# Layer 1 with VectorE's instructions in source order, the closing chain and the token steps cut into pieces

## The chip, the cores and the metric

The kernel runs on one core of a Trainium2 chip. A core has four compute engines with a queue each: TensorE (PE in the profile; its weight loads are shown apart as PEld), VectorE (DVE), ScalarE (ACT) and GpSimd (POOL). SyncE (SP) issues the DMA transfers. TensorE reads operands from SBUF and writes PSUM, from where VectorE and ScalarE read. The metric is the device time of one execution of the whole program in microseconds.

## The reference

Four layers are applied to x, four images of 56 x 56 tokens with 256 channels. Each is `x = x + layer(group_norm(x))`. Layers 0, 2 and 3 are window attentions with 8 heads and are not touched. Layer 1, on the N = 3136 tokens of an image, is cut here to what matters (W_adj is diagonal):

```
xn   = x / norm(x)                              # per token
A    = exp(5 * (xn W_adj xn^T - rowmax))        # N x N, diagonal set to 0
A    = A / rowsum(A);   rowsum = sum(A)
diff = rowsum * (x W_aff + b_aff) - (A x) W_aff
y    = leaky_relu(layer_norm(diff) * gamma + beta, 0.01)
```

All is float32.

## The kernel before

`layer1` works image by image. The tokens of an image are 24 tiles of 128 (`NB`) and a rest of 64 (`REST`). They are made ready in seven chunks: six of four tiles and one for the rest (chunk 6, `NC4`). For a chunk, `tokens` returns a list of steps:

- `load`: the DMA of the chunk, two `normalise` operations on VectorE (L939, group norm, one per half of the channels), a square on ScalarE (L1368).
- `lengths`: sixteen one-column matmuls that sum the squares (L1376); VectorE clips the sum into `rn` (L1378), GpSimd raises it to the power -1/2 (L1379) and spreads it over a diagonal `dg` (L1380).
- two `values` steps: x W_aff into `xw` (L1389), evacuated by ScalarE or VectorE (L954, L952). A last column of xw holds -1, so that the same product gives the row sums.
- `unit_length`: a matmul with `dg` (L1397) and a VectorE product into `xnT` (L1399).

A is symmetric but for its normalisation, so only the blocks on and above the diagonal are computed. A unit `(b, j, first, last)` is row tile j against up to four column tiles. `logits` gives 1 to 4 tiles by matmul (L1421), ScalarE's exp (L1424) and on the diagonal a GpSimd mask (L1426); it runs one unit ahead of the products. `transposed` transposes the tiles on TensorE (L1491) and copies them on ScalarE (L1494). `products` then uses each tile twice: `by_row` (L1505) adds to row j's sum in the PSUM tile `ps_o`, `by_column` (L1510) makes the part of row i in a `ps_v` tile, of which there are two, and `add_up` adds it to `acc` in SBUF on VectorE (L1433; the first time a copy, L1436). Units whose j is None are rest units: the 64 rest tokens against 1024 tokens, with the same scheme on 64-row halves (L1443, L1462, L1472, L1476).

When row j is complete, `finish` closes it, an operation at a time: VectorE adds `ps_o` and `acc` (L1540), takes a reciprocal (L1544), combines (L1546), takes mean and variance (L1549 to L1551); GpSimd raises to a power (L1553); VectorE normalises (L1554); GpSimd applies gamma and beta (L1555, L1556); VectorE applies the leaky ReLU (L1557). It returns `add`, which transposes y on TensorE (L1562) and adds it to the residual (L1570); a full residual chunk gets its statistics (L894) and is stored.

Around the units runs a list `small`. After every unit's products `done` grows by its number of tiles, and twice per unit `small_step` runs the first entry that has come due, or a step of the group statistics. `replace` is called at seven row tiles of an image (j = 3, 6, 10, 14, 18, 20, 22) and puts a chunk of the next image into `small`: its load at once, its other steps eight tiles later. `now` runs all steps of a chunk that a unit is about to need.

`run` opens a layer under a manual schedule for a set of engines. For layer 1 that set holds TensorE alone: TensorE executes in the order of the source, and a scheduler decides how VectorE, ScalarE, GpSimd and SyncE order their own instructions. The first image's chunks are prepared in a loop ahead of the first unit. Layer 2's first loads (`layer2_ahead`) are issued during layer 1.

Of the kernel before, what the change touches and what calls it, by code (L numbers as in the profile page):

```python
# [830 lines left out]
def direct_blocks(ctx: ExitStack, tc: tile.TileContext, d: dict, watch):  # L831
# [501 lines left out]
    def layer1(early, big, pool, late, next_layer):  # L1333
# [16 lines left out]
        def tokens(b, c, ps_a=ps_m):  # L1350
# [6 lines left out]
            def load():  # L1357
                x = early.tile([P, CC, 512], FP, tag="x", name="x1")
                if c < NC4:
                    nc.sync.dma_start(out=x[:, :, :n], in_=tokens_of(1, b, 4 * c * P, n))  # L1360
                else:
                    for i in range(2):
                        nc.sync.dma_start(out=x[:, :, i * REST:(i + 1) * REST], in_=tokens_of(1, b, NB * P, REST))
                x1 = box["x"] = early.tile([P, CC, 512], FP, tag="xn", name="xn1")
                sq = box["sq"] = x
                for h in range(CC):
                    normalise(x1[:, h, :n], x[:, h, :n], known(1, b), h)
                nc.scalar.activation(sq[:, :, :n], x1[:, :, :n], AF.Square)  # L1368

            def lengths():  # L1370
                pm, sq = ps_a(), box["sq"]
                rn = early.tile([P, 4, 1], FP, tag="rn", name="rn")
                dg = box["dg"] = early.tile([P, 4, P], FP, tag="dg", name="dg", bufs=1)
                for i, t in enumerate(tiles):
                    for h in range(CC):
                        nc.tensor.matmul(pm[:k, i:i + 1], lhsT=sq[:, h, i * P:i * P + k], rhs=ones[:, 0:1],  # L1376
                                         start=(h == 0), stop=(h == CC - 1))
                nc.vector.tensor_scalar_max(rn[:k, :m, 0], pm[:k, :m], TINY * TINY)  # L1378
                nc.gpsimd.tensor_tensor(rn[:k, :m, 0], rn[:k, :m, 0], mhalf[:k, 0:1].to_broadcast([k, m]), ALU.pow)  # L1379
                nc.gpsimd.tensor_tensor(  # L1380
                    dg[:k, :m, :k], ident[:k, :k].rearrange("p (o q) -> p o q", o=1).to_broadcast([k, m, k]),
                    rn[:k, :m, :].to_broadcast([k, m, k]), ALU.mult)
# [22 lines left out]
            return [load, lengths] + [lambda i=i: values(i) for i in range(0, m, 2)] + [unit_length]  # L1405
# [23 lines left out]
        touched = set()  # L1429
# [36 lines left out]
        def rest_products(b, q, e, own, at):  # L1466
            po = psum_tile("o", 2)
            for i in range(4):
# [6 lines left out]
                for a in range(2):  # L1475
                    nc.tensor.matmul(po[a * REST:(a + 1) * REST, :C + 1], lhsT=at[:, i * P + a * REST:i * P + (a + 1) * REST],  # L1476
                                     rhs=xw[:, 8 * q + 4 * a + i, :], start=(i == 0), stop=(i == 3 and (a == 1 or own is None)))
            if own is not None:
                nc.tensor.matmul(po[:REST, :C + 1], lhsT=own, rhs=xw[:REST, NB, :], start=False, stop=True)
# [17 lines left out]
        def products(b, j, first, last, e, at):  # L1497
# [18 lines left out]
            for n, i in enumerate(others):  # L1516
                by_column(i)
                if n:
                    by_row(rows.pop(0))
            for i in rows:  # L1520
                by_row(i)
# [3 lines left out]
        def residual(b, c):  # L1525

            if (b, c) not in xr and c < NCH:
                xr[b, c] = late.tile([P, CC, CH], FP, tag="xr", name="xr1", bufs=3)
                nc.sync.dma_start(out=xr[b, c], in_=tokens_of(1, b, c * CH, CH))
            return xr.get((b, c))  # L1530

        def finish(b, j):

            n = P if j < NB else REST
            y = late.tile([P, C + 1], FP, tag="y", name="y", bufs=5) if j < NB else y_rest
# [12 lines left out]
            mv = pool.tile([P, 2], FP, tag="mv", name="mv1")  # L1548
# [3 lines left out]
            rstd = pool.tile([P, 1], FP, tag="rstd", name="rstd")  # L1552
            nc.gpsimd.tensor_tensor(rstd[:n], mv[:n, 1:2], mhalf[:n, 0:1], ALU.pow)  # L1553
            nc.vector.tensor_scalar(y, y, mv[:n, 0:1], rstd[:n], ALU.subtract, ALU.mult)  # L1554
            nc.gpsimd.tensor_tensor(y, y, gamma[:n], ALU.mult)  # L1555
            nc.gpsimd.tensor_tensor(y, y, beta[:n], ALU.add)  # L1556
            nc.vector.scalar_tensor_tensor(y, y, 0.01, y, ALU.mult, ALU.max)  # L1557

            def add():
# [5 lines left out]
                while t0 < j * P + n:  # L1565
# [9 lines left out]
                    t0 = t1  # L1575
            return add
# [16 lines left out]
        for c in range(2):  # L1593
            fresh[c].pop(0)()
        for c in range(NC4 + 1):
            for step in fresh[c]:
                step()
            if c + 2 <= NC4:
                fresh[c + 2].pop(0)()
        small, done = [], 0  # L1600

        def small_step():
            for i, (when, step, _) in enumerate(small):
                if when <= done:
                    small.pop(i)
                    return step()
            step_stats()

        def now(chunk):

            for item in [a for a in small if a[2] == chunk]:
# [3 lines left out]
        def replace(b, c):  # L1615
            if b < NIMG:
                for item in [a[2] for a in small if a[2]]:
                    now(item)
                load, *steps = tokens(b, c)
                load()  # L1620
                small[:0] = [(done + 8, step, (b, c)) for step in steps]
# [10 lines left out]
        for k, w in enumerate(units):  # L1632
# [19 lines left out]
            else:  # L1652
                products(*w, e, at)
                done += w[3] - first
                if w[3] == NB:
                    adds = [finish(b, j)] + ([last_add] if j == NB - 1 else [])
                    small += [(done + 6, add, None) for add in adds]
            e = ahead
        return [step for _, step, _ in small]
# [418 lines left out]
    with pool_of(2, 0) as early, ExitStack() as ends:  # L2078
        late = ends.enter_context(pool_of(1, 3))
        held = {}  # L2080
        last_steps = run(1, lambda own: layer1(*own, late, lambda: layer2_ahead(early, held)), {E.PE}, range(3))
# [101 lines left out]
```

## Time and profile before

| | |
|---|---|
| median of 3 runs | 4060.51 us (4051.37 to 4060.95) |
| the profiled execution | 4046.79 us, span 4044.6 us |
| layer 0 up to | about 795 us of the span |
| layer 1, first image's chunks | 795 to about 848 us |
| layer 1, units | 848 to about 2805 us |
| TensorE busy from 870 to 2803 us | 1888.64 of 1933 us |
| VectorE busy from 870 to 2803 us | 850.06 us |
| ScalarE, GpSimd busy there | 404.40, 464.02 us |
| share of DMA there | 0.06 |

In a profile line, `L1433 DVE` is an operation of VectorE at line 1433 of the kernel. A timeline line has the start, the time to the last end, the engine, the line, the operation with its tiles, the count, and in brackets the idle time of the engine ahead of it with the work that ended it. A line of waits has who waited for whom, the total in us, the number of times and the longest one. In a line of windows, the figures after the two bounds are the length, and then the busy time of PE, PEld, DVE, ACT and POOL with the number of instructions in brackets, the share of full clock that TensorE was granted, the busy share of the DMA engines and GB/s.

### The profile page before, as it was taken

How to read it: one execution, taken by the hardware profiler on the slowest of the kernel's cores; microseconds unless marked ns; L12 is line 12 of the kernel's file. 1: busy time of each engine (PE TensorE's matmuls, PEld its weight loads, DVE VectorE, ACT ScalarE, POOL GpSimd, SP SyncE). 2: the span in 40 equal slices, each digit the busy share in tenths (PEclk: the TensorE clock that was granted, in tenths of full speed). 3: DMA queues.
4: the chain of work that ended last, by engine and by line, in shares of the span. 5: the costliest groups of instructions: out<-in, count | busy, mean ns of one | idle time of the engine just before them, and what ended most of it. 6: DMA issues, size and time to landing. Idle time of an engine off the chain costs nothing.

```text
span 4044.6 us, 92225 instructions
## 1 busy us (share of the span) xinstructions
PE 3858.0 (95%) x38983; PEld 2715.6 (67%) x38983; DVE 2364.8 (58%) x4427; ACT 1375.9 (34%) x2899; POOL 1741.2 (43%) x1883
## 2 busy tenths in 40 slices
PE   6999999899999999999999999999999999999998
PEld 4566666557777577775777757776676676666665
DVE  6777777634444444444344543445788877666665
ACT  3355555322222122222222212222555555344443
POOL 2566767621123211232112321123676777545544
PEclk9899999899999999999999999999999999999999
DMA  8443333320000000000000000001444443322221
GB/s 266 102 133 121 114 118 105 104 85 6 24 23 29 25 6 24 15 29 25 6 24 15 29 19 10 10 10 50 126 128 131 125 119 113 102 73 73 74 77 62
DMA packets 241072, 276.12 MB, mean 68 GB/s; under 512 B 23430, under 2 KB 233000, under 8 KB 240168
## 3 DMA queue, kind: packets, MB, share of 16 engines
q1 hardware_dynamic: 240362, 270.06, 21.5%
q8 instruction: 308, 5.05, 0.5%
q14 instruction: 114, 0.93, 0.1%
q10 hardware_dynamic: 288, 0.08, 0.0%
HBM read 190.55 MB, written 79.53 MB: 67 GB/s over the span
## 4 chain that ended last, share of the span: by engine, by line
PE 48%; DVE 4%; POOL 2%; issue 1%; SPq 0%; DMA 0%; ACT 0%; DVEq 0%; POOLq 0%; ACTq 0%
PE ps_m L945 12%; PE ps_o L1505 6%; PE ps_s L1421 6%; PE ps_v L1510 6%; PE ps_o L1100 3%; PE ps_m L962 3%; PE ps_s L1071 3%; PE ps_o L1040 2%; PE ps_m L982 2%; PE ps_t L1491 1%; PE ps_s L1025 1%; DVE rs L1796 1%; PE ps_m L1389 1%; DVE xn L939 0%; DVE e L1078 0%
## 5 line engine op out<-in xcount | busy, mean ns | idle before, releaser
L1433 DVE TENSOR_TENSOR acc<-acc,ps_v 128x257 f32<-128x257 f32 x1104 | 455.8, 421 | 686.5 <-PE ps_v L1510 671.7
L1510 PE MATMUL ps_v<-xw,e 128*128 128x257 f32 x2208 | 613.1, 382 | 19.7 <-DVE acc L1433 18.0
L1505 PE MATMUL ps_o<-xw,at 128*128 128x257 f32 x2208 | 609.0, 379 | 0.0
L1421 PE MATMUL ps_s<-xnT,xd 128*128 128x512 f32 (+3 forms) x1344 | 571.1, 547 | 0.0
L1494 ACT COPY at<-ps_t 128x512 f32<-128x512 f32 (+3 forms) x332 | 170.5, 514 | 1049.8 <-PE ps_t L1491 1049.8
L1510 PEld LDWEIGHTS ps_v<-xw,e 128*128 128x128 f32 x2208 | 408.6, 189 | 171.1 <-issue 80.4
L1091 POOL TENSOR_TENSOR b<-e 126x336 f32<-126x336 f32 (+5 forms) x512 | 500.0, 997 | 10.0 <-ACT e L1079 1.9
L1505 PEld LDWEIGHTS ps_o<-xw,at 128*128 128x128 f32 x2208 | 419.1, 190 | 60.1
L1414 POOL TENSOR_SCALAR xd<-xnT,vec 128x128 f32<-128x128 f32 x192 | 115.1, 610 | 632.2 <-PE ps_s L1421 629.7
L945 PE MATMUL ps_m<-xn,w_wqkv 128*128 128x392 f32 x1024 | 381.6, 507 | 3.9 <-DVE xr L1831 2.5
L1082 POOL TENSOR_TENSOR e<-e,m0t 126x672 f32<-126x672 f32 (+3 forms) x128 | 238.7, 1865 | 265.0 <-ACT e L1081 252.1
L1082 POOL TENSOR_TENSOR e<-e,bias 119x784 f32<-119x784 f32 (+5 forms) x128 | 244.4, 1909 | 180.9 <-ACT e L1081 179.7
L1421 PEld LDWEIGHTS ps_s<-xnT,xd 128*128 128x128 f32 x1344 | 225.5, 191 | 134.8 <-issue 126.2
L1424 ACT ACTIVATE e<-ps_s 128x512 f32<-128x512 f32 x336 | 185.3, 551 | 336.7 <-PE ps_s L1421 336.7
L1003 ACT ACTIVATE no<-rs 128x168 f32<-128x168 f32 (+2 forms) x256 | 93.9, 367 | 590.2 <-DVE rs L1796 273.2
L945 PEld LDWEIGHTS ps_m<-xn,w_wqkv 128*128 128x128 f32 x1024 | 190.0, 192 | 127.5 <-ACT pr L2028 17.2
L1100 PEld LDWEIGHTS ps_o<-e,vp 124*32 124x32 f32 (+3 forms) x8192 | 176.3, 110 | 141.6 <-issue 93.0
L1100 PE MATMUL ps_o<-e,vp 124*32 124x112 f32 (+3 forms) x8192 | 238.8, 253 | 6.2 <-POOL e L1082 4.4
L939 DVE TENSOR_SCALAR xn<-x,gst 128x28 f32<-128x28 f32 (+5 forms) x368 | 208.1, 619 | 35.2 <-PE ps_m L945 28.7
L1079 ACT ACTIVATE e<-e 126x672 f32<-126x672 f32 (+5 forms) x256 | 219.5, 857 | 19.0 <-DVE e L1078 6.0
L1796 DVE RECIPROCAL rs<-ps_o 128x196 f32<-128x196 f32 (+2 forms) x128 | 176.0, 1375 | 77.7 <-PE ps_o L1100 77.1
L1032 POOL TENSOR_TENSOR e<-e,m3l 98x784 f32<-98x784 f32 x64 | 118.2, 1846 | 235.7 <-ACT e L1029 212.5
(197 smaller groups left out, 6340.9 us busy)
## 6 DMA issues: line engine op xcount, KB each, us to landing
x<-xr SPq DMA_DIRECT2D x64, 392.0 KB
x<-in_x SPq DMA_DIRECT2D x53, 448.0 KB
x<-x SPq DMA_DIRECT2D x60, 392.0 KB
xr<-x SPq DMA_DIRECT2D x60, 392.0 KB
vd<-v SPq DMA_DIRECT2D x48, 384.0 KB
xr<-in_x SPq DMA_DIRECT2D x32, 392.0 KB
xr<-x SPq DMA_DIRECT2D x28, 448.0 KB
x<-xr SPq DMA_DIRECT2D x28, 448.0 KB
```

The costliest lines, as they stand in the source:

```text
L939: nc.vector.tensor_scalar(dst, src, gst[:, h, 0:1], gst[:, h, 1:2], ALU.subtract, ALU.mult)
L945: nc.tensor.matmul(pm[:, :n], lhsT=w[:, h, col:col + P], rhs=rhs(h), start=(h == 0), stop=(h == CC - 1))
L1079: nc.scalar.activation(ev, ev, AF.Exp)
L1082: nc.gpsimd.tensor_tensor(parts(ev), parts(ev), w["emask"], ALU.mult)
L1091: nc.gpsimd.tensor_tensor(w["b"][a][:nk, :, :2 * nq].rearrange("p h (i c) -> p h i c", i=2), ev[:, :, :, 0, :], ev[:, :, :, 1, :], ALU.add)
L1100: nc.tensor.matmul(w["o"](k, i)[j * HD:(j + 1) * HD], lhsT=ones[:nk, :HD] if k else v(j, u), rhs=w["b"][j // 2][:nk, j % 2, i * nq:(i + 1) ...
L1421: nc.tensor.matmul(s[:, :n], lhsT=xd[j][:, h, :], rhs=xnT[:, h, first * P:last * P], start=(h == 0), stop=(h == CC - 1))
L1424: nc.scalar.activation(e[:, :n], s[:, :n], AF.Exp, scale=5.0)
L1433: nc.vector.tensor_tensor(acc[:, i, :], acc[:, i, :], pv[:, :C + 1], ALU.add)
L1505: nc.tensor.matmul(out[j][:, :C + 1], lhsT=e[:, col(i)] if i == j else at[:, col(i)], rhs=xw[:, i, :], start=(i == j), stop=(i == NB - 1))
L1510: nc.tensor.matmul(pv[:, :C + 1], lhsT=e[:, col(i)], rhs=xw[:, j, :], start=True, stop=True)
L1796: nc.vector.reciprocal(rs.rearrange("p (t c) -> p t c", t=2), pv[:, :, 1, :])
```

## The change

VectorE joins the set of engines in layer 1 that execute in source order. Two kinds of work are cut into closures for that:

- `finish` stops after the power. The rest of its chain becomes two closures, `normal` (VectorE, two GpSimd operations) and `leaky` (VectorE), put into `due` for two and five ticks later. `leaky` then puts `add` into `small`.
- `tokens` returns three lists: the load, the two `normal(h)` (the second with the square), and the other steps. `replace` puts four empty steps and the two `normal(h)` into `ticks`.

`tick` is called after every off-diagonal tile in `products` and after every tile of a rest unit. It runs at most one thing: the first entry of `due` that is due, else the first of `ticks`. `ready` runs what is left of a chunk's `normal(h)` when another step of that chunk is about to run, and `settle` closes rows whose buffers are wanted. The buffers of `mv` and `rstd` grow to seven. In the first image, a chunk's `normal(h)` are called directly ahead of its `lengths`, where `load` had them two chunks ahead.

```diff
-                x1 = box["x"] = early.tile([P, CC, 512], FP, tag="xn", name="xn1")
-                sq = box["sq"] = x
-                for h in range(CC):
-                    normalise(x1[:, h, :n], x[:, h, :n], known(1, b), h)
-                nc.scalar.activation(sq[:, :, :n], x1[:, :, :n], AF.Square)
+                box["x"] = early.tile([P, CC, 512], FP, tag="xn", name="xn1")
+
+            def normal(h):
+                normalise(box["x"][:, h, :n], box["x0"][:, h, :n], known(1, b), h)
+                if h:
+                    nc.scalar.activation(box["x0"][:, :, :n], box["x"][:, :, :n], AF.Square)
...
-            return [load, lengths] + [lambda i=i: values(i) for i in range(0, m, 2)] + [unit_length]
+            return [load], [lambda h=h: normal(h) for h in range(CC)], [lengths] + [lambda i=i: values(i) for i in range(0, m, 2)] + [unit_length]
...
+        def settle(tile):
+
+            while open_tiles and open_tiles[0] <= tile:
+                add = next((a for a in small if a[2] == -1), None)
+                if add:
+                    small.remove(add)
+                    add[1]()
+                else:
+                    due.pop(0)[1]()
+
+        def tick():
+            nonlocal ticked
+            ticked += 1
+            if due and due[0][0] <= ticked:
+                due.pop(0)[1]()
+            elif ticks:
+                ticks.pop(0)()
...
                 by_column(i)
                 if n:
                     by_row(rows.pop(0))
+                tick()
...
+                if NCH * b + c >= 3:
+                    b3, c3 = divmod(NCH * b + c - 3, NCH)
+                    settle((b3, min(((c3 + 1) * CH - 1) // P, NB - 1)))
...
-            nc.vector.tensor_scalar(y, y, mv[:n, 0:1], rstd[:n], ALU.subtract, ALU.mult)
-            nc.gpsimd.tensor_tensor(y, y, gamma[:n], ALU.mult)
-            nc.gpsimd.tensor_tensor(y, y, beta[:n], ALU.add)
-            nc.vector.scalar_tensor_tensor(y, y, 0.01, y, ALU.mult, ALU.max)
+
+            def normal():
+                nc.vector.tensor_scalar(y, y, mv[:n, 0:1], rstd[:n], ALU.subtract, ALU.mult)
+                nc.gpsimd.tensor_tensor(y, y, gamma[:n], ALU.mult)
+                nc.gpsimd.tensor_tensor(y, y, beta[:n], ALU.add)
+
+            def leaky():
+                nc.vector.scalar_tensor_tensor(y, y, 0.01, y, ALU.mult, ALU.max)
+                if j < NB:
+                    small.append((done + 3, add, -1))
...
+            due.extend([(ticked + 2, normal), (ticked + 5, leaky)])
+            due.sort(key=lambda a: a[0])
...
         for c in range(NC4 + 1):
-            for step in fresh[c]:
+            for step in fresh[c][1] + fresh[c][2]:
                 step()
...
+        def ready(chunk):
+            for step in normals.pop(chunk, []):
+                if step in ticks:
+                    ticks.remove(step)
+                    step()
...
-                load, *steps = tokens(b, c)
+                (load,), normals[b, c], steps = tokens(b, c)
                 load()
+                ticks.extend([no_step] * 4 + normals[b, c])
                 small[:0] = [(done + 8, step, (b, c)) for step in steps]
...
-                    adds = [finish(b, j)] + ([last_add] if j == NB - 1 else [])
-                    small += [(done + 6, add, None) for add in adds]
+                    finish(b, j)
             e = ahead
+        while ticks or due:
+            tick()
...
-        last_steps = run(1, lambda own: layer1(*own, late, lambda: layer2_ahead(early, held)), {E.PE}, range(3))
+        last_steps = run(1, lambda own: layer1(*own, late, lambda: layer2_ahead(early, held)), {E.PE, E.DVE}, range(3))
```

## The prediction

> **What bounds the kernel now.** I read the page's busy row first, then layer 1's stretch (from about 795 to 2805 us) by windows, then TensorE's waits in it, then the timeline at the places where it waits.
>
> ```profile
> PE 3858.0 (95%) x38983; PEld 2715.6 (67%) x38983; DVE 2364.8 (58%) x4427; ACT 1375.9 (34%) x2899; POOL 1741.2 (43%) x1883
> ...
> 1180.00:1380.00 200.00, 190.36 (x853) 134.96 (x852) 95.25 (x254) 41.66 (x82) 67.95 (x104) 0.97 0.09 28
> 1380.00:1580.00 200.00, 197.11 (x871) 143.57 (x870) 83.66 (x218) 41.63 (x74) 33.44 (x54) 0.99 0.04 13
> 1580.00:1780.00 200.00, 199.30 (x883) 149.39 (x882) 90.60 (x232) 43.49 (x80) 50.18 (x78) 1.00 0.07 22
> ```
>
> In a window the second figure is TensorE's busy time, the fraction after the five engines its granted clock. Layer 1 is bound by TensorE: the middle of an image has it busy 199 of 200 us. What is lost lies where one image ends and the next begins (three times).
>
> ```profile
> PE ps_v L1510 <- DVE acc L1433: 18.0, 25, 1.5
> PE ps_v L1472 <- DVE acc L1436: 11.7, 9, 1.6
> PE ps_v L1472 <- DVE acc L1433: 8.5, 8, 2.1
> PE ps_m L1397 <- POOL rstd L1553: 3.0, 3, 1.0
> PE ps_v L1510 <- DVE mv L1551: 1.7, 4, 0.4
> PE ps_t L1491 <- ACT e L1424: 0.9, 3, 0.3
> PE ps_o L1505 <- POOL e L1426: 0.3, 1, 0.3
> ```
>
> These rows, for 870 to 2803 us, are all of TensorE's idle time there: 44.1 us, nearly all for an accumulation on VectorE (L1433, L1436) that hands back one of two `ps_v` buffers. A second loss follows from the first:
>
> ```profile
> 1327.73 0.70 PE L1472 MATMUL ps_v<-xw,e 64*128 64x257 f32 x4 [1.60 <-DVE acc L1436]
> 1328.36 0.71 PE L1476 MATMUL ps_o<-xw,at 128*64 128x257 f32 x4
> 1329.79 1.23 PE L1472 MATMUL ps_v<-xw,e 64*128 64x257 f32 x4 [0.73 <-DVE acc L1436]
> ...
> 1334.22 3.58 PE L1376 MATMUL ps_m<-ones,x 128*128 128x1 f32 x16
> ```
>
> After 2.3 us of idling the same work takes twice as long: sixteen length matmuls 3.58 us, against 1.84 us at 1307 and 819 us. Window length times (1 - clock) over 880 to 2780 us is 24 us: 6 each in the 200 us from 1180, 1780 and 2180 (clock 0.97), 2 each in those from 1380 and 2380 (0.99), 2 in 880 to 980 (0.98). So the layer loses 44 + 24 = 68 us, and no reordering of VectorE can win more in its body.
>
> [...] accumulations wait behind L1554 and L1557. So the built order tells who waits.
>
> **The change, part by part.** All durations are from this trace. TensorE issues a 257-column product (two records) in 0.43 us; VectorE's accumulation takes 0.42.
>
> *The closing chain (removed waits).* Today L1554 stands right after L1551 and waits for GpSimd's power, and L1557 one accumulation later waits for two GpSimd operations (0.72 each); VectorE idles 61 + 124 us there. After a tile with a full logits block (1.72 us) that is hidden; after short blocks it isn't (1.06 us at 1286.6, 1.49 at 1297.4, 1.60 + 0.73 at 1327.7, 1.61 at 1353.7, 2.08 at 1412.2). In the changed stream two accumulations precede L1554's piece and three more L1557's: GpSimd's 0.57 us and 1.45 us fit, and one 0.4 us piece fits the 0.45 us that TensorE's 0.87 us per accumulation leaves. What I keep: seven waits of 0.35 us beside the residual additions and their statistics, 0.3 at each of four rest units where a piece lies between accumulations, 0.6 at three rest units behind an xnT write, 1.2 for ACT and POOL: 6.6 us. **Removed: 44.1 - 6.6 = 37.5 us idle, and the 24 us of clock.**
>
> *The token steps (added waits).* `load` no longer normalises. The two normalise pieces wait behind four empty ticks and the chain's pieces, and `ready` runs what is left when the chunk's lengths are due. In the stream as built they lie directly ahead of the lengths for all 21 chunks that are prepared during another image:
>
> ```
> acc, leaky, acc, acc, normalise h0, normalise h1, [lengths on TensorE], rn
> ```
>
> On TensorE the lengths (L1376) come directly after the last products of that block. So it waits for VectorE's pair and ScalarE's square, which today are done blocks earlier. The start of the layer shows this chain already once:
>
> ```profile
> 824.45 1.02 PE L1397 MATMUL ps_s<-dg,ones 128*128 128x512 f32 x2
> 828.84 2.10 PE L1376 MATMUL ps_v<-ones,x 128*128 128x1 f32 x16 [3.37 <-ACT x L1368]
> ...
> 825.51 1.22 DVE L1399 TENSOR_TENSOR xnT<-xn,ps_s 128x1024 f32<-128x1024 f32 x1 [0.17 <-PE ps_s L1397]
> 826.65 1.91 DVE L939 TENSOR_SCALAR xn<-x,gst 128x512 f32<-128x512 f32 x4
> ...
> 827.73 1.06 ACT L1368 ACTIVATE x<-xn 128x1024 f32<-128x1024 f32 x1 [1.41 <-issue]
> ```
>
> From the end of the VectorE work ahead: 0.96 (two normalises) + 0.12 + 1.06 + 0.05, less 0.08 overlap = 2.1 us. In a block: the last product ends, 0.05 + 0.42 accumulation, 2.1: 2.6 us, plus 0.17 by which a record's end trails its issue; TensorE covers 0.87 with two row products. Wait: 1.9 us. Chunks 0, 1, 2, 5: 1.9 each; chunk 3, after an L1554 piece in a short block, 2.15; chunk 4, after a rest unit's racc copy with no row products as cover, 2.8; chunk 6 (0.6 and 0.42 us pieces) 0.95. Sum 13.5 per image, **three images: +40.5 us**. Behind the waiting matmuls stand transposes and logits, and ScalarE and GpSimd wait for those.
>
> *The start of the layer.* VectorE in source order does chunk c+1's normalises only after chunk c's xnT. So every chunk there gets the 3.37 us gap that chunk 4 has now. Chunk 0's pair also slides behind layer 0's last residual (ends 801.6; today it ran at 794.4): its lengths start about 803.9 instead of 800.2, +3.6. Chunks 1, 2, 3, 5: 4 x 3.37 = 13.5, less chunk 1's old 0.45; chunk 6, whose pieces are short (1.22 xnT + 0.6 + 0.42 and steps): 2.3, less 1.9 of its old 2.27 us wait for dg, as its rn no longer queues behind xnT: +0.4. Idle: +17. Chunk 4's busy stretch now lasts 828.84 to 836.88 = 8.0 us against 6.1 for chunk 3: 1.9 us of clock per gap, five new gaps: +9.5. **Start: +26.5 us.** Moved DMAs: wqkv (0.8 MB) and the first bias half (3.0 MB) go ahead of chunk 2's load on SP. With 331 GB/s, as in 805 to 815 us, they drain by about 816, chunk 2 is wanted after 820: hidden; if not, a few us. Its exponentials (6 x 0.98) then stand ahead of chunk 2's square on ScalarE and end at about the same moment: 0 to 1 us.
>
> *Clock at the new waits.* Not shown today: 1.9 us idle, then 1.7 us of one-column matmuls. Lengths alone did not halve the clock (1307 us), 1.49 us idle among full products (1297) neither, 1.6 among 64-row ones did (1327). I take 0.7 of the 15 ordinary big gaps at 1.8 us: 19 us (bounds 0 and 27), and 4.5 us for each chunk 4, which sits in sparse work: 13.5 (bounds 0 and 20). **+32.5 us.**
>
> *Remainder.* Deferred pieces of the last three tiles stand ahead of layer 2's first L986: +1 (0 to 3). Order of instructions in layers 0, 2 beyond its first steps, and 3 is as before: 0. Residual additions come some three key tiles later, each still directly behind its transposes on TensorE, and their stores are not wanted before layer 2; `settle` brings an L1554 piece and its L1557 piece together nowhere in the body: 0. The larger mv and rstd pools hold bytes, no time.
>
> **Sum:** -37.5 - 24 + 26.5 + 40.5 + 32.5 + 1 = +39 us. The profiled execution took 4046.8 us (span 4044.6), under the lowest of the three runs shown; 39 us more is 4085.8 there, and 4099.5 on their median of 4060.5.
>
> **Rivals.** (A) As above, 4099, own range 4078 to 4122: 0.68. (B) Gaps under 2 us never trip the clock: without the 32.5, +6.5: 4067; for it 1297 us, against it 1412 us: 0.12. (C) Faster: the chunk pairs are covered. The place is the pair ahead of L1376; its price is 73 us of idle and clock, and it decides below 34 us, 1.9 us per big chunk in all. Covered fully: -34, 4026. For it: VectorE is 58% busy and idles 672 us for ps_v; against: the order leaves no accumulation between pair and lengths. 0.06. (D) [...] start +11, chunks +39: 4149; 1327 us shows a long one, 828 us a short one: 0.12. (E) Both orders run alike, 4060: 0.02, since the streams differ at every closing tile.
>
> **How the numbers follow.** About 0.3% (12 us) is what a measurement of this kernel tells from no change. Slower by more: most of A, D, a third of B: 0.83. Within: most of B, E: 0.11. Faster: C: 0.06. The range 4064 to 4128 takes A with its bounds and most of B; it leaves out C and most of D.
>
> **What would show it.** L1376 waiting for the square at L1369 of the changed file 18 times for 1.7 to 2 us and 3 times near 2.7 within the body, and about six gaps of 3.4 us before 870 us; waits of L1510 and L1472 for accumulations down from 38 us to under 7; the rest units at full clock until chunk 4's lengths; logits of the first image starting some 25 us later. The forecast is wrong if the square waits are short, or if the clock stays full behind them.

## The result, and the profile after

| | before | after |
|---|---|---|
| median of 4 runs each | 4055.94 us (4046.64 to 4060.95) | 4111.99 us (4107.06 to 4126.61) |
| ratio after/before | | 1.0155, 95% interval 1.0137 to 1.0173 |
| the profiled execution | 4046.79 us | 4107.95 us |
| its span | 4044.6 us | 4106.1 us |

The changed kernel is 1.6% slower: 56 us on the medians, 61.5 us between the two profiled executions. Lines of the changed file lie some 20 to 30 further down: L1376 is now L1377, L1368 is L1369, L1380 is L1381, L1389 is L1390, L1397 is L1398, L1399 is L1400, L1421 is L1422, L1433 and L1436 are L1454 and L1457, L1443 is L1464, L1472 is L1493, L1491 is L1513, L1505 is L1527, L1510 is L1532, L1553 and L1554 are L1583 and L1586, L1555 and L1556 are L1587 and L1588, L1557 is L1591, L1562 is L1598, L1570 is L1606. In fill and fill_mid they lie up to two lines further.

From the page of the kernel after, the busy row and its two costliest groups (busy time, mean of one in ns, idle time of the engine ahead of it and its main releaser):

```profile
PE 3889.5 (95%) x38983; PEld 2747.6 (67%) x38983; DVE 2374.0 (58%) x4427; ACT 1376.9 (34%) x2899; POOL 1738.5 (42%) x1883
...
L1454 DVE TENSOR_TENSOR acc<-acc,ps_v 128x257 f32<-128x257 f32 x1104 | 462.9, 422 | 830.9 <-PE ps_v L1532 802.7
L1532 PE MATMUL ps_v<-xw,e 128*128 128x257 f32 x2208 | 611.6, 381 | 3.3 <-DVE acc L1454 2.1
```

TensorE's busy share is the same 95% and hides everything. Its busy time is 31 us longer for the same instructions (3889.5 against 3858.0): work at half clock (mean granted clock 0.971, before 0.978). The second and third row say that the chain half of the change worked: TensorE now waits 2.1 us for L1454 ahead of L1532 in the whole kernel.

TensorE's waits after, first in the body of layer 1 (895 to 2857 us), then at its start (795 to 895 us): what waited for what, us in total, times, longest.

```profile
PE ps_m L1377 <- ACT x L1369: 38.4, 21, 3.0
PE ps_m L1598 <- DVE xnT L1400: 3.9, 3, 1.3
PE ps_m L1398 <- POOL rstd L1583: 3.0, 3, 1.0
PE ps_v L1532 <- DVE acc L1454: 2.1, 6, 0.3
PE ps_m L1598 <- DVE xr L1606: 1.5, 3, 0.5
PE ps_v L1532 <- DVE acc L1457: 1.2, 3, 0.4
```

```profile
PE ps_v L1377 <- ACT x L1369: 22.7, 7, 3.5
```

The waits for accumulations, 38 us before, are 3.3 us. One row has taken their place: the lengths wait for the square, 21 times in the body and 7 times at the start.

The windows view of one image's length and of the start, first before, then after (TensorE's busy time is the second figure, its granted clock the fraction behind the five engines):

```profile
795.00:870.00 75.00, 66.61 (x314) 44.42 (x314) 27.78 (x59) 22.85 (x35) 21.91 (x27) 0.88 0.38 138
1000.00:1509.00 509.00, 496.12 (x2209) 361.74 (x2208) 225.01 (x588) 106.81 (x200) 124.29 (x193) 0.98 0.07 21
```

```profile
795.00:870.00 75.00, 54.58 (x196) 42.65 (x195) 18.60 (x34) 14.77 (x17) 15.12 (x18) 0.75 0.34 129
1000.00:1509.00 509.00, 492.21 (x2166) 358.55 (x2165) 222.95 (x578) 105.70 (x196) 122.30 (x191) 0.98 0.07 21
```

At the start TensorE gets 196 matmul records done where it did 314, with 20 us of idle time for 8 and a clock of 0.75 for 0.88. In an image it is idle 16.8 us for 12.9.

I cut each profiled execution at two moments: the first logits of the remaining tokens (L1464 of the changed file, 848.4 us before, 882.3 after) and the first matmul of layer 2 (L982, 2806.5 before, 2863.1 after). For each stretch I add TensorE's idle gaps, and the time for which the trace's clock record shows half clock (half of it is lost, if TensorE is busy: in the kernel before, sixteen length matmuls took 3.58 us in it for 1.84). All kernels of this study in one table, profiled executions, us:

| kernel | until L1464 | body to L982 | idle in body | at half clock in body | L982 to the end |
|---|---|---|---|---|---|
| before | 848.4 | 1958.1 | 46.2 | 57.1 | 1238.0 |
| after | 882.3 | 1980.8 | 52.4 | 87.4 | 1243.0 |
| start_undo | 859.8 | 1970.9 | 52.4 | 66.3 | 1238.3 |
| early2 | 889.6 | 1939.9 | 32.7 | 45.8 | 1240.8 |
| fill | 878.6 | 1948.5 | 19.7 | 14.3 | 1240.2 |
| sched_dve | 851.9 | 1957.9 | 53.8 | 35.5 | 1247.2 |
| best0 | 858.9 | 1908.2 | 14.1 | 21.6 | 1239.2 |
| best0late12 | 859.5 | 1924.1 | 25.0 | 28.3 | 1244.1 |
| chain_back | 883.0 | 2223.7 | 238.3 | 175.7 | 1238.4 |
| fill_mid | 886.9 | 2003.3 | 52.4 | 102.0 | 1241.1 |
| dense_len | 880.5 | 1952.8 | 52.5 | 27.3 | 1246.2 |

So the change cost 33.9 us up to L1464, 22.7 in the body and 5.0 behind it. The last is no effect of the change that can be told: with the same orders behind layer 1, the last column runs from 1238 to 1247. The first lengths, too, began between 800 and 817 us in these runs (the latest in fill, behind products that it adds).

The timeline shows how one length waits, at chunk 1 of the second image. TensorE first, then VectorE, then ScalarE:

```profile
1206.65 1.03 PE L1527 MATMUL ps_o<-xw,at 128*128 128x257 f32 x4
1209.33 1.95 PE L1377 MATMUL ps_m<-ones,x 128*128 128x1 f32 x16 [1.65 <-ACT x L1369]
1211.13 0.63 PE L1513 MATMUL ps_t<-ident,e 128*128 128x128 f32 x4
1211.60 1.41 PE L1422 MATMUL ps_s<-xnT,xd 128*128 128x256 f32 x4
1212.81 3.24 PE L1390 MATMUL ps_m<-w_waff,xn 128*128 128x256 f32 x8
...
1206.85 0.42 DVE L1454 TENSOR_TENSOR acc<-acc,ps_v 128x257 f32<-128x257 f32 x1 [0.44 <-PE ps_v L1532]
1207.19 1.00 DVE L939 TENSOR_SCALAR xn<-x,gst 128x512 f32<-128x512 f32 x2
...
1208.22 1.06 ACT L1369 ACTIVATE x<-xn 128x1024 f32<-128x1024 f32 x1 [3.37 <-DVE xn L939]
```

Accumulation, the pair of normalises, square, lengths: a chain of four steps over three engines, most of it with nothing on TensorE beside it. TensorE's last product ends at 1207.68, its next work starts at 1209.33. And L1390, eight records, takes 3.24 us behind it, where 1.89 is its time at full clock (chunk 2, at 1291.16 us).

### The profile page after: what moved, and what is told of

It reads as the page before. It is cut to its first block, busy times and chain, and to the rows that moved or that the text cites. A ratio compares the mean times of both kernels' runs of the same rounds, so it can differ in the third digit from the quotient of the medians.

```text
span 4106.1 us, 92244 instructions
## 1 busy us (share of the span) xinstructions
PE 3889.5 (95%) x38983; PEld 2747.6 (67%) x38983; DVE 2374.0 (58%) x4427; ACT 1376.9 (34%) x2899; POOL 1738.5 (42%) x1883
## 5 line engine op out<-in xcount | busy, mean ns | idle before, releaser
L1454 DVE TENSOR_TENSOR acc<-acc,ps_v 128x257 f32<-128x257 f32 x1104 | 462.9, 422 | 830.9 <-PE ps_v L1532 802.7
L1532 PE MATMUL ps_v<-xw,e 128*128 128x257 f32 x2208 | 611.6, 381 | 3.3 <-DVE acc L1454 2.1
L1527 PE MATMUL ps_o<-xw,at 128*128 128x257 f32 x2208 | 609.0, 379 | 0.0
L1422 PE MATMUL ps_s<-xnT,xd 128*128 128x512 f32 (+3 forms) x1344 | 584.3, 558 | 0.0
L1532 PEld LDWEIGHTS ps_v<-xw,e 128*128 128x128 f32 x2208 | 413.7, 189 | 145.8 <-issue 80.4
L1527 PEld LDWEIGHTS ps_o<-xw,at 128*128 128x128 f32 x2208 | 419.1, 190 | 60.1
L1422 PEld LDWEIGHTS ps_s<-xnT,xd 128*128 128x128 f32 x1344 | 229.4, 194 | 138.7 <-issue 130.0
```

The lines of the kernel that those rows point to most:

```text
L1422: nc.tensor.matmul(s[:, :n], lhsT=xd[j][:, h, :], rhs=xnT[:, h, first * P:last * P], start=(h == 0), stop=(h == CC - 1))
L1454: nc.vector.tensor_tensor(acc[:, i, :], acc[:, i, :], pv[:, :C + 1], ALU.add)
L1527: nc.tensor.matmul(out[j][:, :C + 1], lhsT=e[:, col(i)] if i == j else at[:, col(i)], rhs=xw[:, i, :], start=(i == j), stop=(i == NB - 1))
L1532: nc.tensor.matmul(pv[:, :C + 1], lhsT=e[:, col(i)], rhs=xw[:, j, :], start=True, stop=True)
```

## The experiments

Theory: the order of VectorE put each pair of normalises directly ahead of its own lengths. The 28 waits that follow, and the half clock that they trip, are all of the loss, while the cut chain is a gain. Rivals: the start is late because of its transfers; the clock falls for the sparse work rather than for the standing still; the scheduler's order and not the pieces decides.

**start_undo: the first image alone put back.**

```diff
         for c in range(2):
-            fresh[c][0].pop()()
+            for step in fresh[c][0] + fresh[c][1]:
+                step()
         for c in range(NC4 + 1):
-            for step in fresh[c][1] + fresh[c][2]:
+            for step in fresh[c][2]:
                 step()
             if c + 2 <= NC4:
-                fresh[c + 2][0].pop()()
+                for step in fresh[c + 2][0] + fresh[c + 2][1]:
+                    step()
```

> The first image alone is put back: each chunk's pair of normalises is issued with its load, two chunks ahead, and not just ahead of its own lengths. Theory (the start lost 17 us of idle time at seven lengths and about 17 us of clock): 34 us below the changed kernel, about 4078 us; no wait of the lengths for the square above 1 us before 880 us; the first logits of the remaining tokens near 848 us instead of 882. If each gap cost only its idle time and the clock falls for other reasons: 17 us below, about 4095. Rival (the start is late because two more transfers are ahead of the first chunks on the queue, or for the new order of the last blocks of layer 0): within 5 us of the changed kernel.

Measured: 4071.1 us, 1.0046 of before (1.0029 to 1.0063), 41 us below the changed kernel. The waits view of its start, 795 to 895 us:

```profile
PE ps_v L1377 <- ACT x L1369: 3.5, 1, 3.5
```

One wait is left of seven, where none above 1 us was expected. It is chunk 0's, at 806.6 us: its pair stands behind layer 0's last residual addition. The kernel before had no wait there; its one of 3.4 us, at chunk 4, is gone. From the first lengths to L1464 it took 49.7 us, against 79.3 after and 48.3 before. So 30 us of the start are the order of the normalises. (Only 22.6 of them show in the table, because layer 0 ended 7 us later in this execution.) The transfers were not wholly hidden here. VectorE's row for chunk 2:

```profile
822.75 1.00 DVE L939 TENSOR_SCALAR xn<-x,gst 128x512 f32<-128x512 f32 x2 [2.03 <-DMA x<-x]
```

Chunk 1's clip stood behind this wait, and TensorE then waited 2.3 us for chunk 1's diagonal. GpSimd was busy with `xd` until 824.8 us, so the share of the transfer in these 2.3 us stays open.

The other 10 us were not expected. They are in the body (1970.9 for 1980.8), whose instructions and idle time are those of the changed kernel (52.4 us both): only the clock differs, 66 us at half for 87. The same waits tripped it less often. I come back to this below.

**early2: the pair two ticks earlier.**

```diff
-                ticks.extend([no_step] * 4 + normals[b, c])
+                ticks.extend([no_step] * 2 + normals[b, c])
```

> Two empty places of four ahead of a pair, so that the pair of normalises runs with two or three accumulations behind it before the lengths. Theory (the 1.7 to 3 us waits at the lengths are the pair's and the square's own time, and they trip the clock): of 38.4 us idle at the lengths some 34 go, and the clock's 39 us in the body with them, minus up to 10 us for accumulations that now wait behind a normalise: 4112 - 34 - 39 + 5 = about 4045 us (4035 to 4055); the windows from 1095 to 2495 us at a clock of 0.99 to 1.00. Rival 1 (the clock falls for other reasons than these gaps): only the idle time goes, about 4078. Rival 2 (the chunk's data is not there yet, and VectorE waits for the transfer with the accumulations behind it): no gain, 4105 to 4125, with waits for the transfer at the normalise.

Measured: 4072.12 us, 1.0042 (1.0027 to 1.0058), 27 us above what the theory expected. The body is 40.9 us shorter than after, by 19.7 us less idle time and 41.6 us less of half clock (20.8 lost): that is the sum. What is missing are waits that stayed. In its waits view (895 to 2857 us):

```profile
PE ps_m L1377 <- ACT x L1369: 17.9, 15, 2.8
PE ps_v L1532 <- DVE acc L1454: 2.9, 9, 0.3
```

Per image 0.48 us is left at chunks 0, 1 and 2, 1.71 at chunk 5 and 2.79 at chunk 4. Chunks 4 and 5 come among rest units and short blocks, where ticks are few and the chain's pieces go first. Early normalises in front of accumulations cost 0.8 us in all. No wait for a transfer appears: rival 2 is out. Chunk 4 also shows this, two of VectorE's rows, then one of GpSimd's:

```profile
1366.38 1.07 DVE L939 TENSOR_SCALAR xn<-x,gst 128x512 f32<-128x512 f32 x1
1367.71 0.53 DVE L939 TENSOR_SCALAR xn<-x,gst 128x512 f32<-128x512 f32 x1
...
1366.44 0.72 POOL L1588 TENSOR_TENSOR y<-y,bc 128x256 f32<-128x256 f32 x1
```

The first normalise took twice as long, 1.07 us for 0.53, beside a GpSimd operation. In the body of the changed kernel, too, all 27 normalises of 512 columns that overlap no GpSimd operation took 0.54 us, and the six that overlap L1587 and L1588 for 0.65 us or more took 0.84 to 0.94. Here the normalise began 0.06 us ahead of L1588. Why one is slower beside the other is not shown.

**fill: keep TensorE busy in the wait.**

```diff
                 pm, sq = ps_a(), box["x0"]
+                for _ in range(2 if ps_a is ps_m else 4):
+                    nc.tensor.matmul(pm[:, :CC * C].rearrange("p (h q) -> p h q", h=CC), lhsT=ones, rhs=w_aff, start=True, stop=True)
```

> Adds work that the result does not use: ahead of the lengths two (in the first image four) matrix products of 512 columns into the same accumulator, which the lengths then overwrite, 0.86 us each. They keep TensorE busy for 1.7 us (3.4 us) of the wait and do not shorten it. Theory (gap and clock are two costs, and the clock falls because TensorE stands still): waits at the lengths of 38 us fall to about 6 while the fillers take 36, so that no idle time is won, but the clock's 39 us in the body and 17 at the start go: about 4056 us (4050 to 4066). Rival (the clock falls for the sparse work itself, 16 one-column products and a weight load each, gap or no gap): 4112 or a little more. Half way, if only the gaps that the fillers cover in full are harmless: chunks 3 and 4 keep theirs, 4065 to 4075.

Measured: 4059.32 us, 1.0014 (1.0004 to 1.0025), 53 us below the changed kernel, with *more* work in it. Its waits in the body and its windows for one image:

```profile
PE ps_m L1379 <- ACT x L1369: 5.7, 6, 1.3
```

```profile
1000.00:1509.00 509.00, 503.10 (x2234) 364.93 (x2233) 227.55 (x591) 107.67 (x200) 125.56 (x196) 1.00 0.07 21
```

The useful work did not start earlier. Idle time in the body fell by 32.7 us, which the fillers filled, and half clock from 87.4 us to 14.3, worth 36.5; the body is 32.3 us shorter. So the clock is a cost of its own, as large here as the waits, and keeping TensorE busy with nothing useful took most of it away.

**sched_dve: the pieces, but the scheduler's order on VectorE.**

```diff
-        last_steps = run(1, lambda own: layer1(*own, late, lambda: layer2_ahead(early, held)), {E.PE, E.DVE}, range(3))
+        last_steps = run(1, lambda own: layer1(*own, late, lambda: layer2_ahead(early, held)), {E.PE}, range(3))
```

> All the pieces stay as they are, but VectorE's order is given back to the scheduler, as in the kernel before; TensorE's order is that of the changed kernel, word for word. The scheduler takes the pairs of normalises ahead and puts the normalise of the closing chain straight behind the variance, where it waits for GpSimd's power. Theory (the order made both the gain in the chains and the loss at the lengths): the waits at the lengths go (38 idle and 39 clock in the body, 34 at the start), the chains' waits come back (37 idle, 24 clock): 4112 - 111 + 61 = about 4062 us, like the kernel before. Rival (the pieces alone, whoever orders VectorE, keep the accumulations from waiting): about 4001. Rival (source order on VectorE is worth more than the pieces): above 4112.

Measured: 4056.07 us, 1.001 (0.9999 to 1.0022): no different from before. Its waits in the body (895 to 2857 us):

```profile
PE ps_v L1532 <- DVE acc L1454: 19.0, 25, 1.5
PE ps_v L1493 <- DVE acc L1457: 12.0, 9, 1.6
...
PE ps_v L1493 <- DVE acc L1454: 6.6, 5, 1.6
```

These are the waits of the kernel before, almost to the number (18.0, 11.7, 8.5). Cutting the chain alone is worth nothing, since the scheduler closes it up again, and the waits at the lengths are gone, since it draws the pairs ahead. Gain and loss both came with the order.

**chain_back: source order, but the chain in one piece.**

```diff
-            due.extend([(ticked + 2, normal), (ticked + 5, leaky)])
-            due.sort(key=lambda a: a[0])
+            normal()
+            leaky()
...
-                    small.append((done + 3, add, -1))
+                    small.append((done + 6, add, -1))
```

> VectorE stays in source order and the token steps as they are, but the closing chain is issued in one piece: normalise, GpSimd's product and sum, and the leaky step straight behind the variance; the transposes that add the result in come at their old distance. Theory (in source order the pieces are what keeps VectorE from standing before GpSimd with accumulations behind it): VectorE is shut to accumulations for about 5.6 us at each of 72 closings (2.0 + 1.0 for the power + 0.4 + 1.75 for GpSimd + 0.4) against TensorE's 4 to 5 us of other work, so 60 to 150 us above the changed kernel, clock included: 4170 to 4260 us. Rival (the pieces add nothing): within 10 us of the changed kernel, 4102 to 4122.

Measured: 4350.59 us, 1.074 (1.0722 to 1.0757), 239 us above the changed kernel and beyond my 60 to 150. Its waits in the body, here 895 to 3106 us:

```profile
PE ps_v L1532 <- DVE acc L1454: 181.2, 83, 5.3
PE ps_m L1398 <- DVE xw L952: 27.6, 9, 4.2
```

The direction holds. My size was short because I gave TensorE 4 to 5 us of other work at each closing; it lost 2.2 us at each of 83 waits, and a diagonal matmul waited 27.6 us more behind the values' evacuation, which I had not counted. The run changed one thing more: with no pieces ahead of them in `tick`, the pairs came earlier, and only nine waits of 0.3 us are left at the lengths. By early2 and best0 this makes a kernel faster, so it does not weaken the reading. In source order the pieces are worth more than four times what the whole change lost.

**fill_mid: a break in the one-column products.**

```diff
                         nc.tensor.matmul(pm[:k, i:i + 1], lhsT=sq[:, h, i * P:i * P + k], rhs=ones[:, 0:1],
                                          start=(h == 0), stop=(h == CC - 1))
+                    for h in range(CC if i == 1 and ps_a is ps_m else 0):
+                        nc.tensor.matmul(pm[:, C:2 * C], lhsT=ones, rhs=w_aff[:, h, :], start=True, stop=True)
```

> Adds two products of 256 columns (0.95 us together, not used by the result) in the middle of the lengths of each chunk but the smallest, behind the wait and not ahead of it: the wait stays as long, the run of one-column products behind it is cut in two. 18 times 0.95 = 17 us more work. Theory 1 (the clock falls because TensorE stands still for 1.6 us and more): half clock in the body as in the changed kernel, about 4112 + 17 = 4129 us. Theory 2 (the standing still and the 1.9 us of one-column products behind it count together as too little work): some of the 15 drops go, half clock in the body under 50 us, 4100 to 4115 us.

Measured: 4135.73 us, 1.0211 (1.0196 to 1.0226), half clock in the body 102 us. This is theory 1's figure (4129, and a little more). But the fillers left long stretches as they were: a wait that began 0.22 us into a window (of the grid shown next) filled it with 2.6 us of wait and one-column products ahead of the fillers. What the falls of the clock have in common showed another way. In the clock record of the changed kernel every stretch at half clock lasts 3.41, 6.83 or 10.24 us, and all its falls and rises lie on one grid of 3.41 us to within 0.01 us. The record before is the same, with stretches up to 13.65 us, and in start_undo and in this run the falls lie on such a grid too. One step of the grid is called a window below. These are the waits of 1.65 us (1.72 at chunk 5) of two runs, by where in its window each began:

| run | chunk | begins so far into its window (three images) | clock falls |
|---|---|---|---|
| after | 0 | 2.93, 1.05, 0.91 | yes, yes, yes |
| after | 1 | 2.39, 2.16, 2.01 | yes, yes, yes |
| after | 2 | 1.94, 1.71, 1.56 | no, no, no |
| after | 5 | 2.26, 2.11, 2.03 | yes, yes, yes |
| start_undo | 0 | 2.16, 2.22, 2.30 | yes, yes, yes |
| start_undo | 1 | 1.62, 1.68, 1.76 | no, no, no |
| start_undo | 2 | 2.89, 2.96, 3.03 | yes, yes, yes |
| start_undo | 5 | 1.71, 1.79, 1.84 | no, no, no |

In the middle of a window the stretch (the wait, then 1.9 us of one-column products) is split evenly between two windows. Earlier or later, one window gets more of it: at least 2.19 us in the 15 cases in which the clock fell, at most 2.12 in the nine in which it stayed. A wait alone does not order the table: 1.65 us all within one window tripped the clock at 1.05 and not at 1.71. Wait and one-column products together do. The windows view on the grid shows one of each in the changed kernel, chunk 1 and chunk 2 as they are prepared for the second image (a row at the chunk's wait, the next, and the one behind it):

```profile
1205.30:1208.65 3.35, 2.38 (x11) 1.75 (x10) 2.33 (x6) 0.43 (x1) 0.00 (x0) 1.00 0.00 0
1208.70:1212.05 3.35, 2.72 (x23) 2.67 (x24) 0.16 (x1) 0.76 (x2) 0.50 (x1) 1.00 0.00 0
1212.15:1215.50 3.35, 3.35 (x10) 2.64 (x9) 0.00 (x0) 0.68 (x2) 2.63 (x4) 0.50 0.56 157
...
1283.80:1287.15 3.35, 1.93 (x9) 1.34 (x8) 1.89 (x5) 0.88 (x1) 0.00 (x0) 1.00 0.02 5
1287.20:1290.55 3.35, 3.17 (x21) 2.63 (x22) 0.16 (x1) 0.50 (x2) 0.94 (x1) 1.00 0.07 6
1290.65:1293.95 3.30, 3.30 (x15) 2.66 (x14) 0.42 (x1) 1.19 (x2) 1.50 (x3) 1.00 0.45 148
```

The profile calls TensorE busy 2.72 of 3.35 us in the window from 1208.70, and yet the next one is at half: most of that busy time was one-column work. The window from 1283.80 has less busy time, 1.93 us, and trips nothing.

**dense_len: the same waits, with wide products behind them.**

```diff
-                        nc.tensor.matmul(pm[:k, i:i + 1], lhsT=sq[:, h, i * P:i * P + k], rhs=ones[:, 0:1],
+                        nc.tensor.matmul(pm[:k, i * P:(i + 1) * P], lhsT=sq[:, h, i * P:i * P + k], rhs=ones,
                                          start=(h == 0), stop=(h == CC - 1))
-                nc.vector.tensor_scalar_max(rn[:k, :m, 0], pm[:k, :m], TINY * TINY)
+                nc.vector.tensor_scalar_max(rn[:k, :m, 0], pm[:k, :m * P].rearrange("p (i q) -> p i q", q=P)[:, :, 0], TINY * TINY)
```

> The changed kernel with the lengths as products of 128 columns and not one (every column holds the same sum, the first is read): the waits ahead of them stay, the 1.9 us behind each wait are no longer sparse work. In the three runs with the same waits the clock falls on a grid of 3.41 us, and a wait of 1.65 us has tripped it where wait and one-column products together fill 2.2 us or more of one grid window (waits that begin up to 1.05 or from 2.0 us into it) and not between (1.4 to 1.97 us: at most 2.1). Theory (one-column products count as standing still): the 1.65 and 1.72 us waits no longer trip the clock wherever they begin, those of 2.5 and 3.0 us still do; half clock in the body from 87 us to 20 to 45; the wider products cost up to 0.4 us more at each of 18 places: 4112 - 25 + 6 = about 4093 us (4083 to 4103). Rival (the wait alone decides, and the place on the grid): waits that begin below 1.05 or above 2.0 us into a window trip it still, half clock in the body 65 to 100 us, 4105 to 4122.

Measured: 4079.65 us, 1.0072 (1.0055 to 1.0089), 32 us below the changed kernel. Its waits in the body, and a length on the timeline:

```profile
PE ps_m L1377 <- ACT x L1369: 38.4, 21, 3.0
```

```profile
1202.28 2.05 PE L1377 MATMUL ps_m<-ones,x 128*128 128x128 f32 x16 [1.65 <-ACT x L1369]
1204.17 0.60 PE L1513 MATMUL ps_t<-ident,e 128*128 128x128 f32 x4
1204.61 1.03 PE L1422 MATMUL ps_s<-xnT,xd 128*128 128x256 f32 x4
1205.47 1.89 PE L1390 MATMUL ps_m<-w_waff,xn 128*128 128x256 f32 x8
```

The waits are those of the changed kernel to the tenth. The twelve waits of 1.65 and 1.72 us began anywhere from 0.40 to 2.97 us into a window, nine of them where one-column products would have made more than 2.2 us of it (0.40 to 1.11, and 2.49 to 2.97), and none tripped it. Those of 2.5 and 3.0 us still did, all six. Half clock in the body fell from 87.4 to 27.3 us. So in these runs a wait of 1.65 or 1.72 us brought half clock with one-column products behind it (9 of 12 in the changed kernel) and not with wide ones (none of 12), and the two rivals, wait alone and wait with its place on the grid, are out. The products themselves took 0.1 us longer per chunk (2.05 for 1.95), not 0.4.

**best0: both ends of the pair's order mended.** The loop of start_undo, and

```diff
-                ticks.extend([no_step] * 4 + normals[b, c])
+                ticks.extend([no_step] * 0 + normals[b, c])
```

> Two edits together: the first image's normalises go with the loads again, and no empty place is left ahead of a pair. Theory (the waits at the lengths and the clock they trip are all that the change lost; two empty places left 17.9 us of waits, nearly 15 of them at chunks 3 and 4 and the last chunks): start 30 us and body some 60 us below the changed kernel, about 4020 us (4010 to 4030), under the kernel before's 4051; fewer than 8 us of waits at the lengths, half clock in the body under 30 us. Rival (an early normalise sits in front of accumulations and gives the time back at TensorE's waits for them): over 4035 us with more than 10 us of waits for accumulations.

Measured: 4009.18 us, 0.9897 (0.9881 to 0.9913): 41 us faster than the kernel before, 103 us than the changed one, and just below the forecast's 4010 to 4030. (Its count of early2's waits was off: chunks 4 and 5 had 13.5 us, chunk 3 none.) Waits in the body (860 to 2763 us), and one image's window:

```profile
PE ps_m L1598 <- DVE xnT L1400: 3.9, 3, 1.3
PE ps_m L1398 <- POOL rstd L1583: 3.0, 3, 1.0
PE ps_v L1532 <- DVE acc L1454: 2.1, 6, 0.3
PE ps_m L1598 <- DVE xr L1606: 1.5, 3, 0.5
PE ps_v L1532 <- DVE acc L1457: 1.2, 3, 0.4
```

```profile
1000.00:1509.00 509.00, 504.93 (x2269) 370.11 (x2268) 232.39 (x602) 109.80 (x205) 128.68 (x200) 1.00 0.07 21
```

This is the list of the changed kernel without its first row: nothing came in its place, and VectorE's earlier normalises cost no accumulation (2.1 and 1.2 us, as after). The body is 49.9 us shorter than before and 72.6 shorter than after.

**best0late12: the lengths a unit later as well.**

```diff
-                small[:0] = [(done + 8, step, (b, c)) for step in steps]
+                small[:0] = [(done + 12, step, (b, c)) for step in steps]
```

> The same as the run with no empty place, and the lengths and what follows them four blocks later. Theory: the lengths of chunks 3 and 4 find their squares done too, and the waits at the lengths fall to nothing: 5 to 10 us below that run, 4010 to 4020 us. Rival (the values and the unit length now meet the next chunk's use or the closing of the next tile): within 5 us of that run or above, with other waits in their place (for the accumulator that the small steps share, or for the unit length).

Measured: 4025.18 us, 0.993 (0.9916 to 0.9943), 16 us above best0. The rival's case, and more of it than it said: there was no wait at the lengths left to remove, and delayed steps met one another. Its first waits in the body:

```profile
PE ps_m L1398 <- DVE xw L952: 6.6, 9, 0.9
PE ps_m L1390 <- ACT xw L954: 4.1, 6, 0.7
PE ps_s L1422 <- DVE xnT L1400: 3.9, 3, 1.3
```

Values and unit length now wait for each other's accumulator, and logits wait for `xnT`.

## Why the prediction was right

It forecast 4099 us, slower, range 4064 to 4128; 4112 was measured. Its sum was +39 us over the kernel before; the profiled executions are 61.5 apart, the medians 56. That 4112 lies only 13 us from 4099 is in part luck: the forecast was laid on a median of 4060.5, and that of the four runs before is 4055.9. The chain of waits that it named, and their places, are what was found; its sizes for the clock were short. By its steps:

- **Removed waits (37.5 of 44.1 us).** Kept are 11.7 us, not 6.6, so 32.4 went. The waits for accumulations fell to 3.3 us as the order said, and chain_back and sched_dve show that pieces and order did it together. Missed: the diagonal product's wait for the power (3.0 us, which the prediction let go with the rest and which stayed to the digit) and a new one, transposes that want the accumulator which the `xnT` product still reads (3.9 us).
- **Token steps (+40.5 us).** Measured 38.4, at the same 21 places. (Its list of signs, 18 waits of 1.7 to 2 us and three near 2.7, does not fit its own working, which has twelve of 1.9, three of 2.15, three of 2.8 and three of 0.95.) Ordinary chunks waited 1.65 to 1.72 for a predicted 1.9, chunk 6 0.61 for 0.95, chunk 4 2.52 for 2.8. Chunk 3 waited 2.99 for 2.15: its pair took 1.70 us instead of 1.00, while L1587 and L1588 ran on GpSimd. This is the slowing beside GpSimd that early2 shows; no run takes the two apart.
- **Start, idle (+17 us).** Measured 16.8 over 720 us to L1464. start_undo, which takes 13.1 of them back, confirms order as the cause; chunk 0's wait stays.
- **Start, clock (+9.5 us).** Mis-sized. Half clock grew from 22.6 to 56.5 us between 720 us and L1464, which is 17 us lost. The prediction charged each new gap 1.9 us, from one short example; behind five of the seven gaps the record shows 6.83 us at half, so 3.4 us lost. Rival D's sum here (9.5 + 11 = 20.5) was the nearer one.
- **Clock at the new waits (+32.5 us).** 15 of 18 big waits tripped it, 78 us at half, 39 lost. The ordinary ones cost 29 for 19 (12 of 15, at 2.4 us each, not 0.7 of them at 1.8), chunk 4's 10 for 13.5. The mechanism in the prediction ("0.7 of the waits") was a guess at what start_undo and dense_len then showed to be, in these runs, a matter of where a wait begins on the grid (15 of 24 waits) and of how sparse the work behind it is (none of 12 with wide products). That 12 of 15 came near 0.7 is luck: the same waits tripped it at 9 of 15 places in start_undo. The old 24 us did go: only 9 of the 87 us at half lie outside these 15 places.
- **Remainder (+1 us).** 5.0 measured behind L982, within what that stretch varies between runs.

So the sum fell short by 22.6 us: 7.5 in the clock at the start, 6.5 in the clock at the lengths, 5 at the waits that stayed, 4 behind layer 1 and 2 in the body that I can't assign, less 2 at the token steps. Rival B (gaps below 2 us never trip the clock) fell with the nine of twelve that did; its price of 4067 also left out chunk 4's 13.5 us, though the prediction had that gap at 2.8 us. Rival C (covered pairs, 4026) described the kernel that best0 made: once the pair stands ahead of accumulations, the change is a gain. Rival D's sum for the lengths (32.5 + 39 us for 21 gaps) is 3.4 us a gap: chunks 3 and 4 lost that (6.83 us at half behind each), the rest did not. The transfers that the start moved were hidden in the changed kernel: its chunk 2 was normalised from 826.67 us on, straight behind `xnT`, with no wait for data. start_undo, which wants chunk 2 earlier, waited 2.03 us for it, and still won 30 us.

## What to carry to other kernels

An engine put into source order takes each instruction where the source has it (here 28 waits at the lengths, 61 us), so a step must be moved there by hand to where its consumer's engine still has other work; count what TensorE can do between producer and consumer, engine by engine, and put the producer that many microseconds ahead. Price a TensorE wait twice, as idle time and as clock (in the body here 38.4 and 39 us at the lengths), and look at what stands behind it: the waits of the changed kernel came with 87.4 us at half clock with one-column products, and with 27.3 with wide ones (dense_len). Where a wait can't be removed, wide products beside it, even ones whose result is not used, kept most of the clock here (fill, 14.3 us at half).

## What the hardware showed beyond what was expected

- A wait of 1.65 to 1.72 us halved the clock at 15 of 24 places in two runs, by where it began in a 3.41 us grid: all that began up to 1.05 us or from 2.01 us into a window, none from 1.56 to 1.94. Even 0.48 us did it, in all three images (early2, chunk 0, half clock from 1112.9, 1611.2 and 2109.6 us), with 1.9 us of one-column products behind it in the same window. In the first of them L1422's four products, from 1113.14 us, took 3.46 us, against 1.88 in the changed kernel at 1289.44.
- Half clock came without any wait, too. Beside products with all 128 rows, the lengths of best0 never brought it (15 places). At chunk 4 they stand among the 64-row products of the rest units, and where they lay in one window with those, half clock followed in two of three images (from 1334.4 and 2310.7 us); where they lay across two windows, it did not. So the 2.12 and 2.19 us of fill_mid's table are measured among full products only; what 64-row products add was not tried apart. The first of the two, on the timeline and in the windows of the grid:

```profile
1332.16 1.95 PE L1377 MATMUL ps_m<-ones,x 128*128 128x1 f32 x16
...
1331.00:1334.35 3.35, 3.35 (x30) 2.46 (x28) 1.01 (x3) 0.37 (x1) 1.10 (x2) 1.00 0.02 5
1334.45:1337.80 3.35, 3.35 (x8) 0.61 (x7) 0.00 (x0) 0.37 (x1) 2.02 (x2) 0.50 0.17 39
```

- One image of the changed kernel takes 511.8 us, 150 windows to within 0.2 us (510.1 from the first to the second at chunks 6 and 0). So its three images meet the grid nearly alike, and a shift of the whole layer by some microseconds (start_undo) changed the body by 10 us.
- A normalise of 0.53 us took 1.07 beside GpSimd's sum (L1588, early2), and 0.84 or 0.94 beside its product and sum in the changed kernel.
